# One scan step for both channel tiles of a pair, in a fused decoder layer

## Chip, cores and metric

The kernel runs on one core of one Trainium2 chip. The metric is the device time of one execution in microseconds (us). One profiled execution of the kernel before the change is at hand.

## The reference

A decoder layer on x of 8 x 512 tokens with 512 features, all in 32-bit floats: a state-space (Mamba) block, a cross-attention block and a mixture-of-experts block, each followed by a residual sum and a layer norm. The change touches the state-space block, which for the part that matters is:

```python
xz = xn @ in_proj_w
x_main, z = jnp.split(xz, 2, axis=-1)
x_main = silu(causal_conv(x_main))                 # 4 taps, 1024 channels
dt, B_ssm, C_ssm = jnp.split(x_main @ x_proj_w, [32, 48], axis=-1)
dt = softplus(dt @ dt_proj_w + dt_proj_b)
dA  = exp(A * dt[..., None])                       # 16 states per channel
dBx = dt[..., None] * B_ssm[:, :, None, :] * x_main[..., None]
h   = dA_t * h + dBx_t                             # along the 512 tokens
y_t = einsum('bdn,bn->bd', h, C_t)
y   = (y + x_main * D_param) * silu(z)
out = res_scale * (y @ out_proj_w) + residual
```

So for each of 1024 channels and 16 states there is a first-order recurrence along the tokens. Then come attention with 16 heads of 32, and 32 experts of which each token takes 4.

## The kernel before, in words

`layers` does everything up to the routing of tokens to experts, `experts` the experts' products, `finish` the last layer norm. Only `layers` is touched.

**Tiling of the recurrence.** The tokens go in chunks of 256 (T), two for each of the eight sequences, 16 chunks in all. The 1024 channels are 8 tiles of 128 partitions, taken as 4 pairs (q). The 16 states go in 4 groups (g) of 4 (NG). Inside a group two states lie on the two halves of the partitions and the channels of a tile are cut in two halves (j); a scan row has T + 1 elements, the first of which carries the state over. `steps` lists (q, g, i) with i, the tile of the pair, innermost: 32 steps k in a chunk, 512 in all.

**One step k** of the main loop issues, in program order: at i = 0 the broadcast loads of B and C for the next group (`bcast`, four DMAs on the SP queue into two tiles of the pool `l_bc`, which has 4); `carry` (L443), a ScalarE copy of the carried state into column 0 of a tile `h` (4 buffers); `decays` (L437), four ScalarE exponentials into one of the two `l_da` tiles, for step k + 1; `scan`: on VectorE the product of dt*x and B (L449, 1024 elements), the scan itself (L453, 1028 elements) and, in the first chunk of a sequence, a copy of the last state (L455). Then come parts of other work, and at the end `collect`: on VectorE the product with C (L470), on TensorE the sums into PSUM (L474).

**Other work.** `do` issues the TensorE part of a piece of other work and puts what follows it into `left`; `settle` issues one more part of each piece that is left, and `dry` all. Fixed steps: the output projection of the chunk before at k = 1, 2 (`back`, 16 matmuls each); the gate's projections at k = 3 to 6 (`gate_x`); `prepare` for the next pair at k = 3, 11, 19, 27; the next chunk's input projection and convolution at k = 12, 15, 18, 21 (`convolve`). The attention and the gate of the sequence before (`units`) are spread over the steps by planned weights. Attention scores and their exponentials share two PSUM tiles (`l_pss`), nearly all other products share two (`l_psm`).

**`prepare`** makes dt of a pair: matmuls, then ScalarE (L402 to L408), then `both`: four VectorE operations (L412 to L415; the last is dtx = dt*x), two ScalarE products of x and D (L418), and eight DMAs on the SP queue (L426) that lay dt and dtx out for the scan. `convolve` makes x of a pair: a ScalarE copy into `xp` (one buffer), the first tap on ScalarE, then six taps on VectorE into `xs` (6 buffers).

**Order.** The tile framework tracks dependencies by buffers, gives each engine an in-order list of instructions, and fills that list when the kernel is built by priority (the order of the program) among what it takes to be ready then. The list of an engine thus follows the program loosely, and at run time strictly.

Of the kernel before, what the change touches and what calls it, by code (L numbers as in the profile page):

```python
# [7 lines left out]
F32 = mybir.dt.float32  # L8
# [3 lines left out]
ALU = mybir.AluOpType  # L12
# [69 lines left out]
def layers(ctx, tc, a, x1d, filld, based, xbuf):  # L82
# [73 lines left out]

    conv_tail = cp.tile([P, CC, 3], F32, name="l_conv_tail")
    state = cp.tile([P, CC, NST // NG, NG], F32, name="l_state")
    nothing = cp.tile([P, NG, 1], F32, name="l_nothing")
    nc.gpsimd.memset(nothing, 0.0)  # L160
    das = [cp.tile([P, NG, T + 1], F32, name=f"l_da{i}") for i in range(2)]
    for da in das:
        nc.gpsimd.memset(da[:, :, 0:1], 0.0)

# [23 lines left out]
        channel_multiplier=0,  # L188
    )

    early = cp.tile([P, SC, E], F32, name="l_early")
    nc.gpsimd.iota(
        early, pattern=[[0, SC], [-1, E]], base=E, channel_multiplier=0, allow_small_or_imprecise_dtypes=True
    )
    first = cp.tile([P, SC, E], F32, name="l_first")
    nc.gpsimd.iota(
        first, pattern=[[0, SC], [CAP, E]], base=-SLOTS, channel_multiplier=0, allow_small_or_imprecise_dtypes=True
    )

    taken = cp.tile([P, SC + 1, E], F32, name="l_taken")  # L200
    nc.gpsimd.memset(taken, 0.0)
# [172 lines left out]
    def bcast(f, g):  # L374

        got = []
        for r0 in (g * NG, NST + g * NG):
            t = bcp.tile([P, NG // 2, T], F32, tag="bc", name="bc")
            for r in range(2):
                n0 = r0 + r * NG // 2  # L380
                nc.sync.dma_start(
                    t[r * HP : (r + 1) * HP], f["scr"][n0 : n0 + NG // 2, :].partition_broadcast(HP)
                )
            got.append(t.unsqueeze(1).to_broadcast([P, 2, NG // 2, T]))
        return got

    def prepare(q, f):
# [8 lines left out]
        def exponentials():  # L396
# [13 lines left out]
            def both():  # L410

                nc.vector.scalar_tensor_tensor(w, w, -1.0, u, ALU.add, ALU.subtract)  # L412
                nc.vector.tensor_tensor(l, l, w, ALU.subtract)
                nc.vector.tensor_tensor(dt, dt, l, ALU.add)
                nc.vector.tensor_tensor(dtx, dt, f["xs"][q], ALU.mult)  # L415
                for i in range(2):
                    c = 2 * q + i
                    nc.scalar.activation(  # L418
                        f["xs"][q][:, i, :], f["xs"][q][:, i, :], AF.Identity, scale=dpar[:, c : c + 1]
                    )  # L420
# [12 lines left out]
    def decays(c, g, dt, da):  # L433

        for n in range(NG):
            j, m = n // 2, n % 2
            nc.scalar.activation(da[:, n, 1:], dt[:, c % 2, j, :], AF.Exp, scale=aneg[:, c, j, g, m : m + 1])  # L437

    def carry(t, c, g):

        last = state[:, c, g].unsqueeze(2)
        h = p3.tile([P, NG, T + 1], F32, tag="h", name="h", bufs=4)
        nc.scalar.copy(h[:, :, 0:1], last if t else nothing)  # L443
        return h

    def scan(t, c, g, dtx, bc, da, h):

        steps = h.rearrange("p (j m) t -> p j m t", j=2)[:, :, :, 1:]
        nc.vector.tensor_tensor(  # L449
            steps, dtx[:, c % 2].unsqueeze(2).to_broadcast([P, 2, NG // 2, T]), bc[0], ALU.mult  # L450
        )
        flat = h.rearrange("p n t -> p (n t)")
        nc.vector.tensor_tensor_scan(flat, da.rearrange("p n t -> p (n t)"), flat, 0.0, ALU.mult, ALU.add)  # L453
        if t < S // T - 1:
            nc.vector.tensor_copy(state[:, c, g].unsqueeze(2), h[:, :, T : T + 1])  # L455

    def collect(c, g, h, bc, py, f):


        if g == 0:  # L460
            for j in range(2):
# [4 lines left out]
                    start=(c % 2 == 0),  # L466
                    stop=False,
                )
        steps = h.rearrange("p (j m) t -> p j m t", j=2)[:, :, :, 1:]
        nc.vector.tensor_tensor(steps, steps, bc[1], ALU.mult)  # L470
        for m in range(NG // 2):
            for j in range(2):
                s = (g, m, c % 2)
# [70 lines left out]
    def choose(b, x2t, pl, st):  # L544
# [19 lines left out]
        gt = gm.tile(square, F32, tag="g_gt", name="g_gt")  # L564
# [458 lines left out]
    for i, (b, t) in enumerate(chunks):  # L1023
# [8 lines left out]
        for k, (q, g, ci) in enumerate(steps):  # L1032
            if ci == 0:
                if (q, g) != (CC // 2 - 1, NST // NG - 1):
                    bcn = bcast(f, (g + 1) % (NST // NG))
                else:
                    bcn = bcast(nf, 0) if after else None
            h = carry(t, 2 * q + ci, g)

            if k + 1 < len(steps) or after:  # L1040
                nq, ng, ni = steps[(k + 1) % len(steps)]
                decays(2 * nq + ni, ng, (f if k + 1 < len(steps) else nf)["ready", nq][0], das[(n + 1) % 2])
            scan(t, 2 * q + ci, g, f["ready", q][1], bc, das[n % 2], h)
            n += 1
            if k % 8 == 0:
                if k:
                    gated(q - 1, f, py)
# [371 lines left out]
```

## Time and profile before

Three timed runs: 5616.44, 5619.11 and 5622.24 us, median 5619.11. The profiled execution took 5620.06 us, of which the span from the first to the last instruction is 5617.3. Busy times of three stretches of the span, by the profile's answer for windows:

| stretch (us) | PE busy | DVE busy | ACT busy | granted PE clock |
|---|---|---|---|---|
| 1500 to 2000 | 439.83 | 451.73 | 281.66 | 0.94 |
| 2000 to 2500 | 437.28 | 453.32 | 285.83 | 0.93 |
| 4200 to 5000 | 799.60 | 469.38 | 222.87 | 1.00 |

PE is TensorE's matmuls, DVE is VectorE, ACT is ScalarE, POOL is GpSimd, SP the engine whose queue issues most DMAs. The first scan starts at 84.1 us, the last at 3722.0 us; what comes after is the end of the routing, the experts and the last norm. Busy time is the union of an engine's instructions. In what follows "idle before" is the time for which an engine stood still just before an instruction, and the releaser is what ended that.

### The profile page before, as it was taken

How to read it: one execution, taken by the hardware profiler on the slowest of the kernel's cores; microseconds unless marked ns; L12 is line 12 of the kernel's file. 1: busy time of each engine (PE TensorE's matmuls, PEld its weight loads, DVE VectorE, ACT ScalarE, POOL GpSimd, SP SyncE). 2: the span in 40 equal slices, each digit the busy share in tenths (PEclk: the TensorE clock that was granted, in tenths of full speed). 3: DMA queues.
4: the chain of work that ended last, by engine and by line, in shares of the span. 5: the costliest groups of instructions: out<-in, count | busy, mean ns of one | idle time of the engine just before them, and what ended most of it. 6: DMA issues, size and time to landing. Idle time of an engine off the chain costs nothing. (4 is left out here: it accounts for less than half of the span.)

```text
span 5617.3 us, 60406 instructions
## 1 busy us (share of the span) xinstructions
PE 4888.6 (87%) x19752; PEld 2725.6 (49%) x19752; DVE 4351.5 (77%) x5738; ACT 2592.2 (46%) x5480; POOL 546.1 (10%) x424
## 2 busy tenths in 40 slices
PE   5667888888888988888888898879899999999994
PEld 3333344434433434443443443333577777777773
DVE  5988888989889998898989899854555655555554
ACT  4454555655556555565545656523122222222223
POOL 0000002001100200200010020010111111111111
PEclk8778999999999999999999999989899999999997
DMA  6777345434534534543463453431444444444444
GB/s 207 215 219 201 99 129 177 128 112 130 189 107 113 190 107 122 177 132 106 124 204 94 125 183 110 115 118 45 137 124 126 124 124 119 125 126 124 120 117 138
DMA packets 560426, 769.83 MB, mean 137 GB/s; under 512 B 135754, under 2 KB 268394, under 8 KB 560112
## 3 DMA queue, kind: packets, MB, share of 16 engines
q1 hardware_dynamic: 522608, 680.70, 40.2%
q0 software_dynamic: 33280, 76.90, 7.0%
q10 hardware_dynamic: 4224, 8.39, 0.4%
q8 instruction: 156, 2.56, 0.2%
q14 instruction: 158, 1.29, 0.1%
HBM read 508.68 MB, written 165.05 MB: 120 GB/s over the span
## 5 line engine op out<-in xcount | busy, mean ns | idle before, releaser
L437 ACT ACTIVATE l_da<-both,l_aneg 128x256 f32<-128x256 f32 x2048 | 888.4, 499 | 801.8 <-DVE h L453 759.7
L453 DVE TENSOR_TENSOR_SCAN h<-l_da,h 128x1028 f32<-128x1028 f32 x512 | 1171.2, 2295 | 48.5 <-ACT h L443 26.4
L474 PE MATMUL py<-h,l_twice 128*64 128x256 f32 x4096 | 628.1, 420 | 217.4 <-DVE h L470 217.3
L449 DVE TENSOR_TENSOR h<-both,bc 128x1024 f32<-128x1024 f32 x512 | 619.2, 1216 | 97.2 <-PE py L474 45.4
L470 DVE TENSOR_TENSOR h<-h,bc 128x1024 f32<-128x1024 f32 x512 | 623.5, 1220 | 6.0
L474 PEld LDWEIGHTS py<-h,l_twice 128*64 128x64 f32 x4096 | 295.3, 147 | 587.6 <-DVE h L470 260.7
L766 PE MATMUL ps_s<-l_ka,l_qa 64*128 64x512 f32 x1024 | 317.1, 699 | 142.9 <-DVE mx L768 142.7
L1199 PE MATMUL ps_h<-xT,w 128*128 128x320 f32 x1536 | 435.6, 433 | 0.0
L1279 POOL DMA_INDIRECT based<-y,xe x160 | 250.5, 1565 | 1317.2 <-ACT y L1302 579.9
L768 DVE TENSOR_REDUCE mx<-ps_s 128x2 f32<-128x1024 f32 x256 | 310.8, 1217 | 83.7 <-PE ps_s L766 82.9
L1220 DVE TENSOR_TENSOR hT<-ps_h,p 128x320 f32<-128x320 f32 x128 | 62.9, 492 | 374.7 <-PE ps_h L1199 374.6
L1199 PEld LDWEIGHTS ps_h<-xT,w 128*128 128x128 f32 x1536 | 292.4, 191 | 118.4 <-issue 0.8
L792 PE MATMUL ps_t<-l_qa,l_ka 64*128 64x512 f32 x1024 | 302.0, 654 | 15.8 <-ACT eT L796 11.9
L796 ACT ACTIVATE eT<-ps_t 128x1024 f32<-128x1024 f32 x256 | 259.1, 1013 | 111.9 <-PE ps_t L792 111.5
L808 PE MATMUL po<-eT,l_va 128*64 128x512 f32 x1024 | 279.2, 623 | 23.0 <-ACT raw L820 19.0
L1199 PE MATMUL ps_h<-t,s 128*128 128x320 f32 x1024 | 286.1, 432 | 0.0
L641 POOL DMA_INDIRECT xbuf<-x2t,dest x128 | 216.7, 1693 | 622.1 <-DVE dest L635 583.7
L305 PE MATMUL ps_z<-xnT,wm 128*128 128x256 f32 x1024 | 246.3, 395 | 31.2 <-DMA wm<-in_in_proj_w 28.4
L503 PE MATMUL po<-wm,zs 128*128 128x512 f32 x512 | 246.7, 634 | 13.0 <-DMA wm<-in_out_proj_w 8.5
L703 PE MATMUL ps_p<-x2T,wa 128*128 128x512 f32 x512 | 244.7, 627 | 11.1 <-DVE hT L883 9.1
L305 PE MATMUL ps_x<-xnT,wm 128*128 128x256 f32 x1024 | 245.3, 393 | 1.4 <-ACT xnT L294 1.1
L305 PEld LDWEIGHTS ps_z<-xnT,wm 128*128 128x128 f32 x1024 | 196.2, 196 | 83.7 <-ACT l_da L437 27.1
(225 smaller groups left out, 7397.0 us busy)
## 6 DMA issues: line engine op xcount, KB each, us to landing
bc<-scr SPq DMA_DIRECT2D x1024, 128.0 KB
w<-in_w SPq DMA_DIRECT2D x96, 1024.0 KB
wm<-in_in_proj_w SPq DMA_DIRECT2D x128, 512.0 KB
xbuf<-zero SPq DMA_DIRECT2D x32, 1362.5 KB
xe<-xbuf SPq DMA_DIRECT2D x32, 1362.5 KB
both<-dt SPq DMA_DIRECT2D x256, 128.0 KB
both<-dtx SPq DMA_DIRECT2D x256, 128.0 KB
wm<-in_out_proj_w SPq DMA_DIRECT2D x64, 512.0 KB
```

The lines of the kernel that those rows point to most:

```text
L305: nc.tensor.matmul(ps[:, i, :], w[:, dc, i * P : (i + 1) * P], f["xnT"][:, dc, :], start=(dc == 0), stop=(dc == DC - 1),)
L437: nc.scalar.activation(da[:, n, 1:], dt[:, c % 2, j, :], AF.Exp, scale=aneg[:, c, j, g, m : m + 1])
L449: nc.vector.tensor_tensor(steps, dtx[:, c % 2].unsqueeze(2).to_broadcast([P, 2, NG // 2, T]), bc[0], ALU.mult)
L453: nc.vector.tensor_tensor_scan(flat, da.rearrange("p n t -> p (n t)"), flat, 0.0, ALU.mult, ALU.add)
L470: nc.vector.tensor_tensor(steps, steps, bc[1], ALU.mult)
L474: nc.tensor.matmul(py[j * HP : (j + 1) * HP, c % 2, :], twice, h[:, j * 2 + m, 1:], start=False, stop=(s == (NST // NG - 1, NG // 2 - 1, 1)),)
L766: nc.tensor.matmul(ps[:, j, :], qa[r, lt * P : (lt + 1) * P], ka[r, :], start=True, stop=True)
L768: return lambda: nc.vector.tensor_reduce(mx[:, lt, :].unsqueeze(2), ps, AX.X, ALU.max) and None
L792: nc.tensor.matmul(ps[:, j, :], ka[r, kc * P : (kc + 1) * P], qa[r, :], start=True, stop=True)
L796: nc.scalar.activation(eT, ps, AF.Exp)
L808: nc.tensor.matmul(po[j * 2 * HD : (j + 1) * 2 * HD, :], va[:, kc, i, j * HD : (j + 2) * HD], eT[:, j, :], start=(kc == 0), stop=(kc == SC ...
L1199: nc.tensor.matmul(ps, w[:, n, r * P : (r + 1) * P], x[:, n, :], start=not more and n == 0, stop=n == 1, skip_group_check=more,)
```

## The change

`decays`, `carry` and the first two parts of `scan` now take both tiles of a pair at once. They run at i = 0 only: one `carry` of 8 states, eight exponentials in one go (for the next pair-step, that is two steps k ahead), one product of 2048 elements, one scan of 2056, one copy of 8 last states. `collect` stays as it was, one tile at a time. The tiles `l_da` are twice as large and still two; `h` is twice as large, with 2 buffers in place of 4. The pool of B and C has 6 tiles in place of 4. `both` keeps dtx where it was and no longer issues the products of x and D; they are a part of their own (`timesD`), one `settle` later. To make room, `xs` has 5 buffers in place of 6, the tile `l` of `prepare` takes the one buffer of `xp`, two gate tiles (`g_eq`, `g_gt`) share a `row` tile, and two constants are kept once and read through a broadcast.

```diff
-    bcp = ctx.enter_context(tc.tile_pool(name="l_bc", bufs=4))
+    bcp = ctx.enter_context(tc.tile_pool(name="l_bc", bufs=6))
...
-    nothing = cp.tile([P, NG, 1], F32, name="l_nothing")
-    nc.gpsimd.memset(nothing, 0.0)
-    das = [cp.tile([P, NG, T + 1], F32, name=f"l_da{i}") for i in range(2)]
+    none = cp.tile([P, 2, NG], F32, name="l_none")
+    nc.gpsimd.memset(none, 0.0)
+    das = [cp.tile([P, 2 * NG, T + 1], F32, name=f"l_da{i}") for i in range(2)]
...
-    early = cp.tile([P, SC, E], F32, name="l_early")
+    early = cp.tile([P, E], F32, name="l_early")
...
+    early = early.unsqueeze(1).to_broadcast([P, SC, E])
...
-            f["xs"][q] = xs = p2.tile([P, 2, T], F32, tag="xs", name="xs", bufs=6)
+            f["xs"][q] = xs = p2.tile([P, 2, T], F32, tag="xs", name="xs", bufs=5)
...
-            l = p1.tile([P, 2, T], F32, tag="l", name="l")
+            l = p1.tile([P, 2, T + 3], F32, tag="xp", name="l")[:, :, 0:T]
...
                 nc.vector.tensor_tensor(dtx, dt, f["xs"][q], ALU.mult)
-                for i in range(2):
-                    c = 2 * q + i
-                    nc.scalar.activation(
-                        f["xs"][q][:, i, :], f["xs"][q][:, i, :], AF.Identity, scale=dpar[:, c : c + 1]
-                    )
...
+                return lambda: timesD
+
+            def timesD():
+                for i in range(2):
+                    c = 2 * q + i
+                    nc.scalar.activation(
+                        f["xs"][q][:, i, :], f["xs"][q][:, i, :], AF.Identity, scale=dpar[:, c : c + 1]
+                    )
...
+    def decays(q, g, dt, da):
+
+        for i in range(2):
+            for n in range(NG):
+                j, m = n // 2, n % 2
+                nc.scalar.activation(
+                    da[:, i * NG + n, 1:], dt[:, i, j, :], AF.Exp, scale=aneg[:, 2 * q + i, j, g, m : m + 1]
+                )
+
+    def carry(t, q, g):
+
+        h = p3.tile([P, 2 * NG, T + 1], F32, tag="h", name="h", bufs=2)
+        nc.scalar.copy(h.rearrange("p (i n) t -> p i n t", i=2)[:, :, :, 0], last(q, g) if t else none)
         return h
 
+    def last(q, g):
+        return state[:, 2 * q : 2 * q + 2, g]
+
+    def scan(t, q, g, dtx, bc, da, h):
+
+        steps = h.rearrange("p (j m) t -> p j m t", m=NG // 2)[:, :, :, 1:]
+        both = [P, 4, NG // 2, T]
         nc.vector.tensor_tensor(
-            steps, dtx[:, c % 2].unsqueeze(2).to_broadcast([P, 2, NG // 2, T]), bc[0], ALU.mult
+            steps,
+            dtx.rearrange("p i j t -> p (i j) t").unsqueeze(2).to_broadcast(both),
+            bc[0].to_broadcast(both),
+            ALU.mult,
         )
         flat = h.rearrange("p n t -> p (n t)")
         nc.vector.tensor_tensor_scan(flat, da.rearrange("p n t -> p (n t)"), flat, 0.0, ALU.mult, ALU.add)
         if t < S // T - 1:
-            nc.vector.tensor_copy(state[:, c, g].unsqueeze(2), h[:, :, T : T + 1])
+            nc.vector.tensor_copy(last(q, g), h.rearrange("p (i n) t -> p i n t", i=2)[:, :, :, T])
...
-        eq = gm.tile(square, F32, tag="g_eq", name="g_eq")
+        both = p3.tile([P, D], F32, tag="row", name="g_eq").rearrange("p (n j g h) -> p n j g h", n=2, j=SC, g=G)
+        eq, gt = both[:, 0], both[:, 1]
...
-            h = carry(t, 2 * q + ci, g)
-
-            if k + 1 < len(steps) or after:
-                nq, ng, ni = steps[(k + 1) % len(steps)]
-                decays(2 * nq + ni, ng, (f if k + 1 < len(steps) else nf)["ready", nq][0], das[(n + 1) % 2])
-            scan(t, 2 * q + ci, g, f["ready", q][1], bc, das[n % 2], h)
-            n += 1
+            if ci == 0:
+                h = carry(t, q, g)
+
+                if k + 2 < len(steps) or after:
+                    nq, ng, _ = steps[(k + 2) % len(steps)]
+                    decays(nq, ng, (f if k + 2 < len(steps) else nf)["ready", nq][0], das[(n + 1) % 2])
+                scan(t, q, g, f["ready", q][1], bc, das[n % 2], h)
+                n += 1
```

More of the change, by code (lines that the diff above doesn't have):

```diff
@@ L189, in layers @@
     )
-    early = cp.tile([P, SC, E], F32, name="l_early")
-    nc.gpsimd.iota(
-        early, pattern=[[0, SC], [-1, E]], base=E, channel_multiplier=0, allow_small_or_imprecise_dtypes=True
-    )
[L195 to L198, printed above, removed]
+    early = cp.tile([P, E], F32, name="l_early")
+    nc.gpsimd.iota(early, pattern=[[-1, E]], base=E, channel_multiplier=0, allow_small_or_imprecise_dtypes=True)
+    early = early.unsqueeze(1).to_broadcast([P, SC, E])
+    first = cp.tile([P, E], F32, name="l_first")
+    nc.gpsimd.iota(first, pattern=[[CAP, E]], base=-SLOTS, channel_multiplier=0, allow_small_or_imprecise_dtypes=True)
+    first = first.unsqueeze(1).to_broadcast([P, SC, E])
     taken = cp.tile([P, SC + 1, E], F32, name="l_taken")
@@ L383, in bcast @@
                 )
-            got.append(t.unsqueeze(1).to_broadcast([P, 2, NG // 2, T]))
+            got.append(t.unsqueeze(1))
         return got
@@ L415, in both @@
                 nc.vector.tensor_tensor(dtx, dt, f["xs"][q], ALU.mult)
-                for i in range(2):
-                    c = 2 * q + i
-                    nc.scalar.activation(
-                        f["xs"][q][:, i, :], f["xs"][q][:, i, :], AF.Identity, scale=dpar[:, c : c + 1]
-                    )
                 f["ready", q] = []
@@ L427, in both @@
                     f["ready", q].append(to)
-            return both
-        return exponentials
[L433 to L443, printed above, removed]
-        return h
-    def scan(t, c, g, dtx, bc, da, h):
-        steps = h.rearrange("p (j m) t -> p j m t", j=2)[:, :, :, 1:]
+                return lambda: timesD
[5 more added lines that the diff above has]
+                    )
+            return both
+        return exponentials
+    def decays(q, g, dt, da):
[8 more added lines that the diff above has]
+        nc.scalar.copy(h.rearrange("p (i n) t -> p i n t", i=2)[:, :, :, 0], last(q, g) if t else none)
+        return h
+    def last(q, g):
[3 more added lines that the diff above has]
+        both = [P, 4, NG // 2, T]
         nc.vector.tensor_tensor(
-            steps, dtx[:, c % 2].unsqueeze(2).to_broadcast([P, 2, NG // 2, T]), bc[0], ALU.mult
+            steps,
+            dtx.rearrange("p i j t -> p (i j) t").unsqueeze(2).to_broadcast(both),
+            bc[0].to_broadcast(both),
+            ALU.mult,
         )
@@ L468, in collect @@
                 )
+        h = h[:, c % 2 * NG : (c % 2 + 1) * NG]
         steps = h.rearrange("p (j m) t -> p j m t", j=2)[:, :, :, 1:]
-        nc.vector.tensor_tensor(steps, steps, bc[1], ALU.mult)
+        nc.vector.tensor_tensor(steps, steps, bc[1].to_broadcast([P, 2, NG // 2, T]), ALU.mult)
         for m in range(NG // 2):
@@ L560, in choose @@
         own = gs.unsqueeze(3).to_broadcast(square)
-        eq = gm.tile(square, F32, tag="g_eq", name="g_eq")
+        both = p3.tile([P, D], F32, tag="row", name="g_eq").rearrange("p (n j g h) -> p n j g h", n=2, j=SC, g=G)
+        eq, gt = both[:, 0], both[:, 1]
         nc.vector.tensor_tensor(eq, other, own, ALU.is_equal)
         nc.vector.tensor_tensor(eq, eq, lower.unsqueeze(1).to_broadcast(square), ALU.mult)
-        gt = gm.tile(square, F32, tag="g_gt", name="g_gt")
         nc.vector.tensor_tensor(gt, other, own, ALU.is_gt)
```

## The prediction

> **What bounds the kernel now.** I read the busy table and the costliest groups first, then the busy time in windows of 20 us, then who waited for whom, and last VectorE's order of time inside one stretch. The chain of waits that ended last covers only the final layer norm (its pieces begin at 5509 us), so it says nothing of the scan.
>
> ```profile
> PE 4888.6 (87%) x19752; PEld 2725.6 (49%) x19752; DVE 4351.5 (77%) x5738; ACT 2592.2 (46%) x5480; POOL 546.1 (10%) x424
> ...
> L437 ACT ACTIVATE l_da<-both,l_aneg 128x256 f32<-128x256 f32 x2048 | 888.4, 499 | 801.8 <-DVE h L453 759.7
> L453 DVE TENSOR_TENSOR_SCAN h<-l_da,h 128x1028 f32<-128x1028 f32 x512 | 1171.2, 2295 | 48.5 <-ACT h L443 26.4
> ...
> L449 DVE TENSOR_TENSOR h<-both,bc 128x1024 f32<-128x1024 f32 x512 | 619.2, 1216 | 97.2 <-PE py L474 45.4
> ```
>
> Over the whole span PE looks like the bound, but the experts fill it. Up to 3700 us, where the scans are nearly over, the windows add up to 3298 us of DVE and 3112 of PE: 89% and 84%. The three VectorE operations of a scan step alone cost 619.2 + 1171.2 + 623.5 = 2414 us. ACT waits 759.7 us for scans before its decays: it runs ahead of DVE and has room. Who is the bound changes every few tens of us:
>
> ```profile
> 1580.00:1600.00 20.00, 15.41 (x76) 5.52 (x76) 19.52 (x17) 11.63 (x26) 0.00 (x0) 1.00 0.24 72
> ...
> 1640.00:1660.00 20.00, 20.00 (x74) 8.41 (x71) 17.46 (x14) 9.08 (x19) 0.00 (x0) 0.99 0.34 112
> 1660.00:1680.00 20.00, 20.00 (x100) 14.16 (x99) 16.89 (x27) 7.94 (x21) 0.00 (x0) 1.00 0.58 181
> ```
>
> The columns are PE, PEld, DVE, ACT, POOL busy, then the granted clock. At 1580 us (attention) DVE is full and PE has a quarter free; at 1640 (output projection and gate) PE is full and DVE waits. Of the 35 windows between 1300 and 2000 us, DVE is at 19 us or more in 18, PE in 12, both in 6. So 12 are DVE's alone, 6 are PE's alone, 17 are both's or nobody's.
>
> ```profile
> ACT h L443 <- PE py L474: 241.6, 146, 5.3
> ...
> ACT xs L418 <- DVE dtx L415: 136.5, 56, 4.5
> ...
> DVE h L449 <- PE py L474: 45.4, 27, 3.7
> ```
>
> Total us, times and longest. The first and third are waits for an `h` buffer: the sums of four steps earlier have to be done before the buffer is written again. They mark where PE is the late one.
>
> ```profile
> 1714.40 2.30 DVE L453 TENSOR_TENSOR_SCAN h<-l_da,h 128x1028 f32<-128x1028 f32 x1
> 1716.74 1.23 DVE L470 TENSOR_TENSOR h<-h,bc 128x1024 f32<-128x1024 f32 x1
> 1717.88 1.22 DVE L768 TENSOR_REDUCE mx<-ps_s 128x2 f32<-128x1024 f32 x1
> 1719.02 1.22 DVE L449 TENSOR_TENSOR h<-both,bc 128x1024 f32<-128x1024 f32 x1
> 1720.34 2.30 DVE L453 TENSOR_TENSOR_SCAN h<-l_da,h 128x1028 f32<-128x1028 f32 x1
> ```
>
> Start and duration. A product whose successor does not need it hands over after 1.14 us (1716.74 to 1717.88); one whose successor needs it, after 1.32 (1719.02 to 1720.34).
>
> **The change, part by part.**
>
> *Fused product.* 512 of 1024 elements become 256 of 2048. Products of 512 elements take 688 ns (L415), of 1024 take 1216: 528 ns per 512 elements, so about 160 ns are fixed. Saved: 256 x 160 = 41 us busy. By hand-over times it is 1.14 - 1.06 = 0.08 us a pair where the next instruction is independent, and 1.32 - 1.06 = 0.26 where it is not: 20 to 67 us. I take 41.
>
> *Fused scan.* No other size of scan is in the trace. At worst all of its 2295 ns grow with size (saved 0); at best the fixed part is the product's plus its hand-over (2.33 us dependent, 1714.40 to 1716.74 above with the start of the next, against 2.14 of size, which is 2295 ns less the 155 below): 0.19. A loss is excluded: two halves cannot have less fixed cost than one whole. I take 155 ns, as it is the same engine and data: 40 us, between 0 and 49.
>
> *Last states.* 256 copies of 166 ns (42.1 us) become 128: 21 us. Column 0 likewise on ACT: 256 of 194 ns gone, 50 us, off the path since ACT is under 60% busy there; without that room it would be 50 us.
>
> Sum on DVE: 41 + 40 + 21 = 102 us, between 41 and 137.
>
> The Trainium skill speaks against the first size: VectorE's page "Vector Engine (DVE) Microarchitecture Reference", section "Measured stream behaviour on trn2", gives about 75 ns per instruction after queue overlap, half of what two durations give here. By it the two fusions would bring an estimated 2 x 256 x 75 ns = 38 us and not 81; the 1.14 us hand-over above is on its side, the 1.32 is not.
>
> *How much of it reaches the end.* All in DVE's own windows (12 of 35), none in PE's own (6), half in the other 17: (12 + 8.5) / 35 = 0.59. 0.59 x 102 = 60 us. Bounds: 0 (PE is the limit throughout) and 102.
>
> [...]
>
> *Two large `h` in place of four small.* The product may start once the sums of both tiles two pair-steps earlier are done. Before, step 2n needed the sums of step 2n - 4; now of 2n - 3 too. DVE can run ahead by half a step less on average. Queued behind the waiting `carry` on ACT are the decays and all evictions of PSUM; behind the waiting product on DVE everything. A step of DVE is 4.8 to 5 us (1.32 + 2.33 + 1.14, with the copy 0.2). Each chunk has one long PE stretch, k = 1 to 6 (1645 to 1681 in the trace). Half a step each time: 16 x 2.5 = 40 us lost. Bounds: 0 (DVE not that far ahead) and a whole step at two stretches a chunk, the second being the convolution: 32 x 5 = 160.
>
> *Eight decays together, a step earlier.* The number is unchanged. They need dt of the next pair at k = 8q + 6, not 8q + 7. ACT already waited for that DMA 38.1 us in 22 places. The wait can grow, and with it the evictions behind; DVE uses the result only after its next scan, so I take 0. A gain is excluded by ACT's room. At most every one of the 64 pairs shows the mean wait of those 22 on the path: 64 x 1.7 = 109.
>
> *Six tiles for B and C.* The SP queue stood 286.4 + 284.7 us at L381 for the two products that free B and C; those waits should nearly vanish, and the DMAs queued behind (dt, weights, x) leave earlier. What the engines waited for such DMAs in the whole run: 26.8 (dtx), 11.2 (B, C), 42.0 (xt) on DVE, 28.4 (wm), 24.8 (xr) on PE, 133 us. Most is latency or bound to other buffers; I take 20, between 0 and 133.
>
> *Product of D and x later.* ACT's 136.5 us of waiting for dtx goes. Late behind it were evictions and first taps; DVE waited for ACT's taps and dt 44.5 + 37.1 us. I take 15, between 0 and 82.
>
> *Room made.* Five `xs`: the buffer taken is that of the pair whose last reader was four steps earlier or more (k = 17 for k = 21), cover is that distance. `l` in the buffer of `xp`: at the `prepare` of k = 19 the Ln waits for six taps (2.7 us on DVE) of the convolution at k = 18; once a chunk, 0 taken, 16 x 2.7 = 43 at most. Gate tiles in a `row` tile: eight times in the run, 0 taken; the two rows are then one short for some 10 instructions. The broadcast constants have the same elements: 0.
>
> Sum: -60 + 40 - 20 - 15 = -55 us. 5620.06 (profiled, 2.8 above its span, 0.95 above the median) - 55 = 5565.
>
> **Rivals.**
>
> *Full saving.* DVE is the real bound nearly throughout, PE's full windows just follow its order. For: 90% busy, and PE waits for DVE in turn (217 us for L470, 143 us for L768). Against: six windows that are PE's alone. Time: 5620 - 102 - 35 = 5483 without the loss at `h`, about 5520 with it.
>
> *The wait for `h` takes over (slower).* Place: `carry` and the product in PE's stretches. A whole step is lost at both stretches of a chunk: +160, against the gains 60 + 35: 5620 + 65 = 5685. It decides from 95 / 32 = 3.0 us lost at a stretch. For: 241.6 + 45.4 us are waited there already, with four buffers, and the double scan (some 4.4 us) delays the first of the two C products by 3.5 us, so the sums come later and in twos. Against: most of these waits are ACT's, which has room.
>
> *PE absorbs it.* Share near 0.2 rather than 0.59, gains and loss cancel: 5610 to 5630.
>
> That the change does not do what it says is excluded for the instruction counts; that other tables get loaded between Silu and the decays is possible (135 loads of 1.28 us now, on ACT), a small change of either sign.
>
> **How the numbers follow.** Part saving 0.42 (5540 to 5605), full saving 0.20 (5480 to 5540), no change 0.08, slower 0.30 (5631 to 5720). No change means within 0.2%, 11 us, about what a measurement can tell here. Faster 0.62, same 0.08, slower 0.30. The range reaches into both outer cases: 5490 to 5665 leaves out about 0.2.
>
> **What would show it.** Right: the scan at 4.40 to 4.45 us x256, the product at 2.27 x256, DVE busy lower by about 100 us; SP's waits at L381 for products small; no ACT wait before L418; DVE's wait for the sums before L449 up by some 40 us. Wrong: that wait, or the scan's wait for `carry`, beyond 140 us more (slower rival); the DVE share up to the last scan at 93% or more (full saving); ACT's waits for dt multiplied with PE waiting for evictions, which I set at nothing.

## The result, and the profile after

| | time, us (median) | span of the profiled execution | last scan starts |
|---|---|---|---|
| before | 5620.41 (4 runs beside it) | 5617.3 | 3722.0 |
| after | 5711.09 (5704.43 to 5713.46, 4 runs) | 5702.7 | 3805.0 |

The change makes the kernel slower: ratio 1.0161, 95% interval [1.0146, 1.0176]. From the last scan to the end it is 1895.3 us before and 1897.7 after, so all of the loss lies in the stretch with the scans. The changed kernel's line numbers differ: product L456, scan L463, product with C L481, its sums L485, `carry` L446, decays L439, the broadcast loads L379, the products of x and D L426.

The busy line of the page, after:

```profile
PE 4923.1 (86%) x19752; PEld 2739.6 (48%) x19752; DVE 4307.6 (76%) x5098; ACT 2487.9 (44%) x5173; POOL 601.0 (11%) x424
```

VectorE has 640 instructions less (256 products, 256 scans, 128 copies) and is busy 43.9 us less than the 4351.5 of before: 69 ns for each. Its groups, as the costliest groups list them (busy and mean ns of one, then idle before):

```profile
L463 DVE TENSOR_TENSOR_SCAN h<-l_da,h 128x2056 f32<-128x2056 f32 x256 | 1135.4, 4435 | 17.1 <-ACT l_da L439 3.5
L439 ACT ACTIVATE l_da<-both,l_aneg 128x256 f32<-128x256 f32 x2048 | 865.6, 497 | 430.4 <-DVE h L463 396.8
...
L456 DVE TENSOR_TENSOR h<-both,bc 128x2048 f32<-128x2048 f32 x256 | 584.1, 2286 | 213.4 <-PE py L485 114.2
L481 DVE TENSOR_TENSOR h<-h,bc 128x1024 f32<-128x1024 f32 x512 | 611.1, 1218 | 5.1
```

The scan group fell by 35.8 us (from 1171.2), the product group by 35.1 (from 619.2), the last states by 20.5 (42.1 to 21.6): 91 together, twice what the engine's busy time fell by. A group adds up whole durations, and the end of one instruction runs beside the start of the next. VectorE in order of time shows it (start, duration, and idle before in brackets):

```profile
1703.23 2.29 DVE L456 TENSOR_TENSOR h<-both,bc 128x2048 f32<-128x2048 f32 x1 [2.85 <-PE py L485]
1705.63 4.44 DVE L463 TENSOR_TENSOR_SCAN h<-l_da,h 128x2056 f32<-128x2056 f32 x1
1709.98 0.67 DVE L410 SCALAR_TENSOR_TENSOR dtx<-dtx,u 128x512 f32<-128x512 f32 x1
1710.57 1.22 DVE L481 TENSOR_TENSOR h<-h,bc 128x1024 f32<-128x1024 f32 x1
1711.70 0.69 DVE L411 TENSOR_TENSOR l<-l,dtx 128x512 f32<-128x512 f32 x1
```

The scan starts at 1705.63 and lasts 4.44, yet its successor, which does not need it, starts at 1709.98, 0.09 us before the scan's end. Every instruction taken away takes such an overlap with it.

So VectorE has less to do and the end comes later. The waits of VectorE up to 3830 us (total us, times, longest):

```profile
DVE h L456 <- PE py L485: 114.2, 60, 3.5
DVE mx L779 <- PE ps_s L777: 63.5, 28, 5.0
DVE xs L337 <- ACT xs L329: 54.2, 30, 7.7
DVE h L456 <- DMA both<-dtx: 53.8, 18, 5.7
DVE m L59 <- ACT r L57: 22.5, 34, 4.2
...
DVE g_m L557 <- PE ps_l L550: 19.6, 7, 3.9
```

The same view of before, up to the last scan there:

```profile
DVE h L449 <- PE py L474: 45.4, 27, 3.7
DVE xs L339 <- ACT xs L331: 44.5, 25, 7.7
DVE st L73 <- DMA xt<-in_x: 42.0, 15, 9.5
DVE zs L486 <- PE py L474: 40.2, 19, 4.3
DVE dtx L412 <- ACT dtx L408: 37.1, 8, 10.1
DVE h L449 <- DMA both<-dtx: 26.8, 15, 7.1
DVE h L453 <- ACT h L443: 26.4, 16, 2.0
...
DVE mx L768 <- PE ps_s L766: 13.1, 10, 2.2
```

The wait for the sums is 114.2 us where it was 45.4. But the five other lines have grown as well, from 13.1 (scores, `mx`), 44.5 (taps, `xs`), 26.8 (dtx), 8.1 (`m`, of a layer norm) and 0.4 (`g_m`, of the gate), together about 121 us more. Four have fallen by about 103 us together: the loads of x (`xt`) to 7.0, the gate (`zs`) to 19.1, dt (`dtx` from ACT) to 15.3 and the `carry` to 1.3. All waits of VectorE up to the last scan add up to 361 us before and 494 after; no single one holds the loss. SP and ACT, in the whole run:

```profile
SPq L379 <- DVE h L481: 451.4, 117, 9.8
...
SPq L379 <- DVE h L456: 218.6, 100, 6.7
```

```profile
ACT l_da L439 <- DVE h L463: 396.8, 112, 8.3
...
ACT h L446 <- PE py L485: 238.9, 120, 9.1
```

The six tiles of B and C have not emptied the SP queue's wait (571 us before, 670 now). ACT still waits for the sums as long as before (241.6), only in fewer and longer pieces. Two of the 20-us windows (PE, PEld, DVE, ACT, POOL busy, then the granted clock):

```profile
1640.00:1660.00 20.00, 16.73 (x74) 5.44 (x74) 18.54 (x12) 11.74 (x24) 0.00 (x0) 0.91 0.44 106
...
1700.00:1720.00 20.00, 20.00 (x102) 13.33 (x100) 14.57 (x21) 9.95 (x22) 0.00 (x0) 1.00 0.63 185
```

In the first neither PE nor VectorE is full, in the second PE is. Of the 35 windows from 1300 to 2000 us, VectorE is at 19 us or more in 10 (18 before) and PE in 10 (12 before). Neither engine is the bound more often than before; both stand still more.

### The profile page after: what moved, and what is told of

The parts are those of the page before. It is cut to its first block, busy times and chain, and to the rows that moved or that the text cites. A ratio compares the mean times of both kernels' runs of the same rounds, so it can differ in the third digit from the quotient of the medians.

```text
span 5702.7 us, 59276 instructions
## 1 busy us (share of the span) xinstructions
PE 4923.1 (86%) x19752; PEld 2739.6 (48%) x19752; DVE 4307.6 (76%) x5098; ACT 2487.9 (44%) x5173; POOL 601.0 (11%) x424
## 5 line engine op out<-in xcount | busy, mean ns | idle before, releaser
L463 DVE TENSOR_TENSOR_SCAN h<-l_da,h 128x2056 f32<-128x2056 f32 x256 | 1135.4, 4435 | 17.1 <-ACT l_da L439 3.5
L439 ACT ACTIVATE l_da<-both,l_aneg 128x256 f32<-128x256 f32 x2048 | 865.6, 497 | 430.4 <-DVE h L463 396.8
L485 PE MATMUL py<-h,l_twice 128*64 128x256 f32 x4096 | 652.4, 424 | 143.9 <-DVE h L481 142.6
L456 DVE TENSOR_TENSOR h<-both,bc 128x2048 f32<-128x2048 f32 x256 | 584.1, 2286 | 213.4 <-PE py L485 114.2
L481 DVE TENSOR_TENSOR h<-h,bc 128x1024 f32<-128x1024 f32 x512 | 611.1, 1218 | 5.1
L485 PEld LDWEIGHTS py<-h,l_twice 128*64 128x64 f32 x4096 | 310.6, 149 | 519.4 <-issue 232.6
L714 PE MATMUL ps_p<-x2T,wa 128*128 128x512 f32 x512 | 264.1, 668 | 25.6 <-DVE hT L894 20.2
L1211 PEld LDWEIGHTS ps_h<-t,s 128*128 128x128 f32 x1024 | 194.6, 190 | 81.1
```

The costliest lines, as they stand in the source:

```text
L439: nc.scalar.activation(da[:, i * NG + n, 1:], dt[:, i, j, :], AF.Exp, scale=aneg[:, 2 * q + i, j, g, m : m + 1])
L456: nc.vector.tensor_tensor(steps, dtx.rearrange("p i j t -> p (i j) t").unsqueeze(2).to_broadcast(both), bc[0].to_broadcast(both), ALU.mult,)
L481: nc.vector.tensor_tensor(steps, steps, bc[1].to_broadcast([P, 2, NG // 2, T]), ALU.mult)
L485: nc.tensor.matmul(py[j * HP : (j + 1) * HP, c % 2, :], twice, h[:, j * 2 + m, 1:], start=False, stop=(s == (NST // NG - 1, NG // 2 - 1, 1)),)
L714: nc.tensor.matmul(ps, lhs(dc), rhs(dc), start=(dc == 0), stop=(dc == DC - 1))
L1211: nc.tensor.matmul(ps, w[:, n, r * P : (r + 1) * P], x[:, n, :], start=not more and n == 0, stop=n == 1, skip_group_check=more,)
```

## Experiments: is it the pair step, or what came with it?

All ratios are to the kernel before, which took 5616 to 5618 us beside them. Theories: R, the rest of the change (room, B and C, product of D) costs the time; H, the two large `h` tiles; D, a fused instruction releases its first half late; I, one scan of 4.4 us that nothing can get into; L, the order of the lists that goes with it. The earlier expectations name two more: G, that the long product and scan, placed together, delay what PE waits for; O, that any edit of the step reshuffles the lists and moves the time by some 50 us without system.

**e1_rest**: the kernel before with every edit but the pair step.

```diff
-    bcp = ctx.enter_context(tc.tile_pool(name="l_bc", bufs=4))
+    bcp = ctx.enter_context(tc.tile_pool(name="l_bc", bufs=6))
...
+                return lambda: timesD
...
-            f["xs"][q] = xs = p2.tile([P, 2, T], F32, tag="xs", name="xs", bufs=6)
+            f["xs"][q] = xs = p2.tile([P, 2, T], F32, tag="xs", name="xs", bufs=5)
```

> The kernel before with every edit of the change but the pair step: five xs, l in the buffer of xp, the gate tiles in a row tile, the two constants read by broadcast, six tiles for B and C, the product of D and x one part later. Theory H (two large h buffers make VectorE wait for the sums) and theory G (the long product and scan, placed together, delay what PE waits for): no slower than before, 5590 to 5630 us; the 35 us that the prediction credited to the SP queue and ScalarE would show as 5585. Theory R (the edits that make room cost the time): 5680 to 5715.

Measured 5597.52 us, 0.9969 [0.9956, 0.9981]. R falls: the rest is a gain of 19 us, and the pair step costs 114.

**e12_bc6**: the kernel before with six tiles for B and C alone (the first pair of lines above).

> The kernel before with six tiles for B and C and nothing else. If e1's 19 us come from the SP queue: 5590 to 5605. If from the product of D and x one part later, or the rest: 5610 to 5620.

5607.18 us, 0.9986 [0.9977, 0.9996]: 9 of the 19 us. The other 10 come with the later product of x and D and the room edits, which were not parted.

**e2_unfused**: the changed kernel, product and scan as two instructions each, in the same place, with the same large `h`.

```diff
-        steps = h.rearrange("p (j m) t -> p j m t", m=NG // 2)[:, :, :, 1:]
...
+        for i in range(2):
+            hi, di = h[:, i * NG : (i + 1) * NG], da[:, i * NG : (i + 1) * NG]
+            nc.vector.tensor_tensor(
+                hi.rearrange("p (j m) t -> p j m t", m=NG // 2)[:, :, :, 1:],
...
+            nc.vector.tensor_tensor_scan(flat, di.rearrange("p n t -> p (n t)"), flat, 0.0, ALU.mult, ALU.add)
```

> The changed kernel, but the product and the scan of the pair are again two instructions of 1024 and 1028 elements each, at the same place in the program and on the same large h tile. VectorE's busy time goes back up by about 40 us. H: still slow, 5720 to 5760, the wait for the sums before the products about 110 us as in the changed kernel. G: the blocks are short again, 5630 to 5680.

5644.68 us, 1.0049 [1.0032, 1.0066]. The two fusions together, which I counted as a gain, cost 66 us. VectorE's busy time is 4318.3 us, 11 above the changed kernel's and not the 40 expected. Yet VectorE waits for the sums nearly as long as in the changed kernel (105.5 us, in the whole run):

```profile
DVE h L457 <- PE py L486: 105.5, 64, 3.2
```

**e3_h4**: e2 with four small `h` tiles, as before the change.

```diff
-        h = p3.tile([P, 2 * NG, T + 1], F32, tag="h", name="h", bufs=2)
+            h = p3.tile([P, NG, T + 1], F32, tag="h", name="h", bufs=4)
```

> As e2, but each tile of the pair has its own h tile, with four buffers, as before the change; carried state and last states are copied for each tile apart. The step is still placed for the pair, eight decays together. H: the wait for the sums before the products falls to 45 us or less and the time to 5620 to 5660. G: as e2 within 15 us.

5643.05 us, 1.0045 [1.0028, 1.0062]: that wait falls to 70.2 us and the time stays. H falls for this arrangement.

**e4_h3** gives the changed kernel a third large `h` (and, to make the room, four tiles of B and C and the `g_oh` tiles in the buffer of `total`); **e8_bc4** makes that room alone and keeps two `h`.

```diff
-        h = p3.tile([P, 2 * NG, T + 1], F32, tag="h", name="h", bufs=2)
+        h = p3.tile([P, 2 * NG, T + 1], F32, tag="h", name="h", bufs=3)
```

> The changed kernel with three large h buffers in place of two; to make room, four tiles for B and C and the four one-hot tiles of the gate in the idle tile total. H: the wait for the sums before the product falls below 40 us and the time to 5560 to 5620, under the kernel before. G: 5690 to 5725, the wait for the sums may fall but others take its place. R: 5690 to 5725.

> The control for e4: the changed kernel with two large h buffers, but with e4's room (four tiles for B and C, the gate's one-hot tiles in total). If e4 lost its 75 us by the third h buffer: 5695 to 5730 here, as the changed kernel. If by the room: 5760 to 5800.

e4: 5785.64 us, 1.0296 [1.0278, 1.0313], far above every range given. e8: 5690.04 us, 1.0135 [1.0118, 1.0152]. The third tile did what it is for, the wait for the sums is 24.5 us; and the time rose by 96 us. VectorE's longest waits up to 3900 us in e4:

```profile
DVE dtx L410 <- ACT dtx L406: 94.3, 29, 10.3
DVE xs L337 <- ACT xs L329: 91.3, 32, 7.4
DVE h L456 <- DMA both<-dtx: 87.0, 32, 8.0
```

VectorE now waits for ACT's part of dt, for the taps and for the DMAs of dt and dtx. A longest wait in a list is no proof that its removal helps. e8 also shows that six tiles of B and C (or the place of the `g_oh` tiles) cost something in the changed kernel, where six were worth 9 us in the kernel before: 21 us by the medians, 15 by the two ratios, whose intervals just overlap.

## Experiments: which fusion?

**e5_prod** keeps the fused product and splits the scan; **e6_scan** keeps the fused scan and splits the product.

```diff
-        nc.vector.tensor_tensor_scan(flat, da.rearrange("p n t -> p (n t)"), flat, 0.0, ALU.mult, ALU.add)
+        for i in range(2):
+            flat = h[:, i * NG : (i + 1) * NG].rearrange("p n t -> p (n t)")
+            di = da[:, i * NG : (i + 1) * NG]
+            nc.vector.tensor_tensor_scan(flat, di.rearrange("p n t -> p (n t)"), flat, 0.0, ALU.mult, ALU.add)
```

> The changed kernel with the product of the pair fused (2048) and the scan as two of 1028 on the same large h. Theory G (the single uninterrupted block of 4.4 us of scan is what costs): near e2, 5625 to 5665. Theory O (any edit of the step reshuffles the lists of the engines, and the time moves by some 50 us without system): anywhere between 5600 and 5720.

> The changed kernel with two products of 1024 and the fused scan of 2056. G: near the changed kernel, 5690 to 5730. If the fused product is what costs: near e2, 5630 to 5660. O: anywhere between 5600 and 5740.

e5: 5595.48 us, 0.9959 [0.9947, 0.9972]. e6: 5738.75 us, 1.0222 [1.0205, 1.0239]. e5 came out below every range given, e6 a little above G's and within O's. From e2, fusing the product is a gain of 49 us (it also puts the two scans next to each other in the program), fusing the scan a loss of 94; on top of the fused product the fused scan costs 116. Splitting that one instruction takes away the whole loss. What does VectorE do up to the end of its last scan? The answers for one window each, first after, then e5 (PE, PEld, DVE, ACT, POOL busy, granted clock):

```profile
0.00:3809.40 3809.40, 3164.14 (x12752) 1518.37 (x12752) 3278.03 (x3174) 1968.99 (x4109) 316.88 (x229) 0.91 0.50 143
```

```profile
0.00:3707.80 3707.80, 3124.25 (x12754) 1508.18 (x12754) 3277.96 (x3435) 1980.12 (x4109) 265.53 (x229) 0.92 0.49 146
```

VectorE is busy 3278 us in both: the fused scan saves nothing, and the 102 us between the two are idle time. On TensorE the same 102 us are 62 of idle time and 40 of longer busy time over the same matmuls. By the clock records of the two traces its granted clock stood at half for 681 us of this stretch after and for 560 in e5 (at full for 3129 and 3148). So the lower clock goes along with the loss; whether it only follows from the idle time or adds to it, no run separates. Why nothing is saved is to be seen in e5's order of time:

```profile
1705.99 4.49 DVE L465 TENSOR_TENSOR_SCAN h<-l_da,h 128x1028 f32<-128x1028 f32 x2
1710.39 1.20 DVE L781 TENSOR_REDUCE mx<-ps_s 128x2 f32<-128x1024 f32 x1
...
1758.04 2.29 DVE L465 TENSOR_TENSOR_SCAN h<-l_da,h 128x1028 f32<-128x1028 f32 x1
1760.25 0.67 DVE L854 SCALAR_TENSOR_TENSOR attT<-attT,total 128x512 f32<-128x512 f32 x1
1760.84 2.29 DVE L465 TENSOR_TENSOR_SCAN h<-l_da,h 128x1028 f32<-128x1028 f32 x1
```

Two scans in a row, which do not need each other, take 4.49 us together, one fused takes 4.44: 0.05 us, 13 us in the whole run at most. And at 1760.25 something stands between the two, the last step of an attention normalization; PE's projection (L716) starts behind it at 1760.97, having stood still for 5.11 us. In e5's trace the two scans of a pair run in a row in 188 of 256 pairs; in the other 68 there is other work between them (144 instructions, 36 of them taps of the convolution, 22 of the chain that makes dtx).

**e9_reversed** is e5 with the scan of the second tile first, so that the first half of `h` comes free as late as in the fused one. **e10_split** is e5 with the eight decays in two lots, as before the change.

```diff
-        for i in range(2):
+        for i in (1, 0):
             flat = h[:, i * NG : (i + 1) * NG].rearrange("p n t -> p (n t)")
```

> e5 with the two scans of a pair in the other order, second tile first. Then, as with the fused scan, the first C product (tile 0) and the first decays of the next pair but one (tile 0's half of l_da) have to wait until both scans are done, but each scan is still an instruction of its own. Theory D (what costs in the fused scan is that everything behind it is released only at the end of 4.4 us): 5680 to 5720. Theory I (what costs is one instruction of 4.4 us in VectorE's list, where nothing else can be put between): 5595 to 5630.

> e5 with the eight decays taken apart again: the next pair's first tile at the first step, the second tile's at the second step. If the lump of decays costs what e7 against e1 showed (34 us): 5550 to 5575. If that was only e7's mix of lumped decays with single steps: 5590 to 5610.

e9: 5618.54 us, 1.0000 [0.9990, 1.0009]: D is worth 23 us of the 116. e10: 5599.28 us, 0.9972 [0.9959, 0.9984], no better than e5.

**e7_decays** is e1 with the eight decays in one lot a step earlier, all else one tile at a time. **e11_prod_only** is e1 with the fused product and two large `h`, scans and decays at their own steps.

```diff
+            if ci == 0 and (k + 2 < len(steps) or after):
+                nq, ng, _ = steps[(k + 2) % len(steps)]
+                decays(nq, ng, (f if k + 2 < len(steps) else nf)["ready", nq][0], das[(n + 1) % 2])
```

> e1 with one edit: the eight decays of the next pair are issued together at its first tile's step, a step earlier than before, into large l_da tiles; products, scans and h stay one tile at a time at their own steps. If the decays in a lump and their earlier need of dt are what the placement costs: 5630 to 5660, as e3. If it is the two scans at one place: 5585 to 5610, as e1.

> e1 with the fused product alone (and with it the large h in two buffers, one carried copy for both tiles); decays, scans and last states stay one tile at a time at their own steps. The fused product's hand-over saving is some 20 to 40 us: 5560 to 5580 if the placement of the product costs nothing; 5600 or more if two large h buffers cost here.

e7: 5631.76 us, 1.0029 [1.0019, 1.0038], 34 more than e1. ACT's wait for the sums before `carry` is 422.5 us there, against 208.0 in e1; its wait for scans before the decays is 297.7 against 759.5. The eight decays now stand ahead of a `carry` in ACT's list; how that costs the 34 us was not traced. e11: 5674.00 us, 1.0099 [1.0082, 1.0116], 77 more than e1: the second branch of its expectation, which e15 tries.

**e15_large_h** is e11 with the product undone.

```diff
-        nc.vector.tensor_tensor(
-            steps,
-            dtx.rearrange("p i j t -> p (i j) t").unsqueeze(2).to_broadcast(both),
...
+        nc.vector.tensor_tensor(
+            h.rearrange("p (j m) t -> p j m t", m=NG // 2)[:, :, :, 1:],
+            dtx[:, c % 2].unsqueeze(2).to_broadcast(both),
```

> As e11_prod_only with the product undone: the kernel of e1, but h for both tiles in two buffers with one carry per pair; products, scans and decays one tile at a time at their own steps. If the two large h are what made e11 slower (+77 us to e1), it is 5650 to 5680 us; if the fused product ahead of its second scan is (it writes the second half eight halves too early and holds VectorE 2.3 us), 5595 to 5615 us.

5681.33 us, 1.0108 [1.0093, 1.0124], 84 more than e1. So the two large `h` (with one `carry` for both tiles) cost 84 us where products and scans stay at their own steps; the fused product on top (e11) changes that by 7 us, which is within the noise. From e2 to e5, where both scans follow it, it brought 49. In VectorE's waits the sums take 106.0 us (78.1 in e1), the scores 140.2 (80.5):

```profile
DVE mx L776 <- PE ps_s L774: 140.2, 58, 28.0
DVE h L453 <- PE py L482: 106.0, 61, 4.8
```

## Experiments: the instruction, or the order around it?

**e13_back_to_back** is e9 with the second scan always right behind the first in VectorE's list; **e14_back_to_back_early** is the same with the first tile's scan first.

```diff
+            if i:
+                nc.vector.tensor_tensor_scan(flat, di, flat, 0.0, ALU.mult, ALU.add)
+                continue
+            with tc.high_priority():
+                tc.keep_in_program_order(nc.vector.tensor_tensor_scan(flat, di, flat, 0.0, ALU.mult, ALU.add))
```

> As e9_reversed (fused product, two scans, that of the second tile first), but the second scan always stands right behind the first in VectorE's list: 256 pairs in 256, where e9 had 189. The lists then agree with those of the changed kernel in 99% of VectorE's places, 97% of ScalarE's and 99% of TensorE's. Theory L (the order of the lists decides): the time is that of the changed kernel less little, 5690 to 5720 us. Theory I (the long instruction itself decides): the time is that of e9, 5610 to 5630 us.

> As e13, with the scan of the first tile first, so that its half is free to be multiplied with C one scan (2.3 us) earlier. Late release was worth 23 us between e5 and e9. Theory L: 5665 to 5700 us. Theory I: as e5, 5590 to 5605 us. If the release is what counts once the lists are those of the changed kernel: near 5600 us here and near 5700 us in e13.

e13: 5683.66 us, 1.0114 [1.0099, 1.0129]. e14: 5668.12 us, 1.0082 [1.0069, 1.0096]. e13 lies a little below the range of theory L (5690 at the low end), e14 inside it, and both are far from theory I as it was stated there. The same instructions of the same durations as in e9 and e5, with the two scans kept together, take 65 and 73 us more. That is more than the seam alone: the build fills the lists otherwise around the pair. Against e9, some 7% of VectorE's and of ScalarE's instructions and 2% of TensorE's stand in another order in e13's trace; for e14 against e5 it is 6, 7 and 2%. The 65 and 73 us are the price of both together. VectorE's waits up to 3830 us, first e5, then e13:

```profile
DVE h L456 <- PE py L487: 91.9, 59, 3.5
...
DVE xs L337 <- ACT xs L329: 38.0, 19, 5.9
DVE h L456 <- DMA both<-dtx: 37.8, 12, 5.5
...
DVE m L59 <- ACT r L57: 11.9, 19, 2.7
```

```profile
DVE h L456 <- PE py L492: 119.8, 66, 3.7
...
DVE h L456 <- DMA both<-dtx: 53.4, 19, 5.8
DVE xs L337 <- ACT xs L329: 47.3, 30, 6.4
...
DVE m L59 <- ACT r L57: 22.3, 36, 4.2
...
DVE g_m L564 <- PE ps_l L557: 18.7, 7, 4.1
```

These lines of e13 are close to those of the changed kernel (114.2, 53.8, 54.2, 22.5, 19.6). Other lines went the other way (`zs` from 48.7 to 22.0), and the view runs 122 us past e5's last scan; up to each kernel's own last scan all waits of VectorE add up to 396 us in e5, 472 in e13 and 494 after. PE shows another side of it, up to 3830 us, in e13:

```profile
PE ps_t L810 <- ACT eT L814: 33.3, 22, 4.1
...
PE py L479 <- DVE v L54: 20.3, 6, 3.4
```

In the changed kernel these are 37.7 and 20.5, in e5 9.5 and nothing: an attention product (`ps_t`) and the start of a new `py` wait longer, by the releasers for exponentials and a small norm step. PE's longest wait, for the products with C, fell meanwhile (180.7 in e5, 151.4 in e13, 142.6 after). So these rows fit the reading that late small work is what suffers; they do not measure it.

**e17_scan_later** moves the fused scan of the changed kernel in the program behind the other work of its step; **e18_both_later** the fused product as well.

```diff
             settle()
+            if ci == 0:
+                run(t, q, g, das[n % 2], h)
+                n += 1
             collect(2 * q + ci, g, h, bc, py, f)
```

> The changed kernel with the fused scan (and the copy of the last states) issued behind the other work of its step, just ahead of the product with C: other work that is ready gets VectorE first. Instructions, buffers and durations are those of the changed kernel. Theory L (order of the lists): the time comes down from 5711 us by a good part of the 65 to 73 us that e13 and e14 showed, 5620 to 5680 us. Theory I (the one long instruction costs by itself, wherever it stands): 5690 to 5720 us.

> As e17 with the fused product moved behind the other work as well. It is later for the scan by one piece of other work where DVE is the late one. Theory L: 5620 to 5690 us; theory I: 5690 to 5730 us.

e17: 5699.66 us, 1.0149 [1.0135, 1.0163]. e18: 5683.74 us, 1.0130 [1.0112, 1.0148]. e17 lies where theory I had it, e18 at the upper end of theory L. Other lists around the fused scan bring 11 and 27 us by the medians (7 and 17 by the ratios, the first within the noise), not the 65 to 73: in the six kernels with it (after, e4, e6, e8, e17, e18) the time is 5684 to 5786 us. That no list would do better is not shown. Read with e13 and e14 (5684 and 5668 us), what these kernels have in common is that nothing can be put between the two halves, be they one instruction or two. The five with a pair step whose list may part the scans (e2, e3, e5, e9, e10) take 5595 to 5645.

**e16_prod_bc4** is e5 with the room of e8 (four tiles of B and C).

> As e5_prod with four tiles for B and C in place of six (and the g_oh tiles in the buffer of total, which makes the room, as in e8). By the sum of e5 (-21 us to before) and e8 (-21 us to after): 5575 us. If the gain of four tiles hangs on the fused scan: 5590 to 5605 us.

5615.77 us, 0.9995 [0.9985, 1.0004], 20 more than e5 and above both expectations. What e8 gained does not carry over. e16 also gives the fused scan a third price: e8 is the same kernel with it, and takes 74 us more, beside the 94 and 116 above. So theory O, changes without system, does not explain the loss, though 74 to 116 shows how much the rest of the kernel moves it. e5 is the fastest kernel found, about 23 us below the kernel before (16 to 30 by the interval); the intervals of e1 and e10 overlap with its own.

The way from before to after, step by step: the rest -19 (e1), the pair step in separate instructions +47 (e2), the fused product -49 (e5), the fused scan +116 (after). (They add up to 95 and not 91, since the kernel before took 5616 us beside e1 and 5620 beside the changed kernel.) The last divides into late release 16 to 23 (e9 to e5, e14 to e13), halves kept together 65 to 73 (e13 to e9, e14 to e5), and 27 that are left between e13 and after.

## Why the prediction was wrong, point by point

The forecast was 5565 us; the result, 5711, is beyond the range too, on the other side of no change. The step that failed is the fused scan: the sum has it as a gain of 40 us on VectorE, of which 0.59 reach the end, with "A loss is excluded". The runs show a loss of 116 us in its place (e5 to after; 94 and 74 in the two other pairs).

- **Fused product, 41 us.** The duration was right (2286 ns against 2.27 us), and the end gained 49 us from it (e2 to e5). VectorE's busy time, though, fell by 11 us only between these two (4318.3 to 4307.6); the other 38 are idle time that went, which my sum had no term for.
- **Fused scan, 40 us, "between 0 and 49".** The 4.435 us lie in the forecast band; the saving is 0.05 us a pair, at most 13 us, and nothing in the busy time of e5 and after. (The upper bound was also read a little low: 1714.40 to 1716.74 is 2.34 us, not 2.33, which makes it 51.) The trace of before already showed the small saving, two scans in a row whose next neighbour starts 4.41 us after the first:

```profile
3680.43 4.49 DVE L453 TENSOR_TENSOR_SCAN h<-l_da,h 128x1028 f32<-128x1028 f32 x2 [2.15 <-ACT l_da L437]
3684.84 1.20 DVE L470 TENSOR_TENSOR h<-h,bc 128x1024 f32<-128x1024 f32 x1
```

This is a mis-sized term, and behind it is the missing one. I had excluded a loss for the fixed cost alone. Most of it comes from keeping the halves together: in 68 of 256 pairs of e5 the list uses the seam between two scans, and closing it, with the lists that follow from that, costs 65 to 73 us of the 116.

- **Sum on DVE, 102 us.** It fell by 43.9 us. The Trainium skill's "Vector Engine (DVE) Microarchitecture Reference", section "Measured stream behaviour on trn2", gives about 75 ns per instruction after queue overlap (measured there on integers); the runs show 69 for the 640 that went, against 159 in my sum (102 us over 640). I saw the 1.14 us hand-over and took the durations all the same.
- **How much reaches the end, 0.59.** Not shown by any run as a share. With 44 us of work gone the time rose by 91, so a share of busy time was the wrong form: the idle time is not fixed.
- **Two large `h`, +40 (0 to 160).** In the pair step it is 0 (e3 to e2), at single steps 84 (e15 to e1). My sign that it would be wrong, a wait of VectorE for the sums "beyond 140 us more", did not show: it rose by 69. And this wait is not where the time goes: e5 has 91.9 us of it and is faster than before, e4 has 24.5 and is slowest.
- **Eight decays, 0 (0 to 109).** Alone 34 us (e7), within the bounds; in the pair step nothing (e10 to e5). The reason "ACT has room" did not hold alone: in e7 its wait before `carry` doubles, and why that reaches the end stays open. The sign I had named, ACT's waits for dt multiplied, did not show (38.1 us before, 21.3 after).
- **Six tiles, -20.** -9 alone (e12), -20 beside the fused product (e16 to e5), 15 to 21 lost beside the fused scan (e8 to after; in the last two the `g_oh` tiles move as well). The reason given failed: SP's waits for the two products did not vanish. They fell from 571 to 454 us in e12 (232.0 + 221.7) and rose to 670 in the changed kernel.
- **Product of D and x, -15.** With the room edits 10 (e1 to e12). ACT's wait did not go, it is 152.2 us against 136.5: the product still meets a dtx that is not there yet.
- **Rivals.** The slower rival gave 5685, nearest to the result, with chance 0.30. Its mechanism, the wait for `h`, is not what costs: in e3 and e4 that wait falls and the time does not. Full saving and "PE absorbs it" fall with e2 and e5, where the parts show gains and losses of 50 to 116 us.

What stays open: the 27 us between e13 and after. VectorE's product waits in the changed kernel for things e13 does not have, the lines "remote" and "issue" (no releaser that the profile shows) and a weight's DMA, 26.5 us in seven places; that this is the same 27 us was not tried. Nor is the 47 us of e2 over e1 settled: decays, carry, products and scans of a pair at once cost it, but e7 and e10 show that the parts do not add up. Each experiment also fills the lists anew, e13 and e14 too; how much of a difference that makes by itself, beside the closed seam, no run separates.

## What to carry to other kernels

Price a fusion by start-to-start times of neighbours that do not need each other, or by the engine's busy union; a difference of mean durations counts the overlap as a saving and gave twice the true value here. Before two long instructions of an in-order engine become one, look what stands between them in the trace, even if only in a quarter of the places: that seam may be where late small work for other engines gets through. And make the parts of such a change one at a time: here one of the two fusions gained 49 us and the other lost more than twice as much.

## What the hardware showed that was not expected

- A scan of 2056 elements takes 4435 ns, of 1028 elements 2289 to 2295; two in a row without a dependency take 4.49 us. Size is nearly the whole price.
- The granted clock and the busy time of PE differ between kernels with the same 19752 matmuls: e10 has 4864.9 us at 0.941, e1 4873.5 at 0.937, after 4923.1 at 0.928, e15 4927.0 at 0.930. It goes along with the time but not strictly, as with the half-clock time of after and e5 above: e2 and e3 take the same time with 4880.3 and 4912.0 us. What of it is cause and what is effect, no run here separates.
- More buffers made the kernel slower twice: a third `h` by 96 us (e4 to e8), and six tiles of B and C with the fused scan by 15 to 21 (after to e8), the latter together with the place of the `g_oh` tiles. With the scan split, the same six tiles were 20 us the better (e5 to e16).
